# A graph attention layer on one NeuronCore: edge mask over three tables, output projection in two passes, layer norm work on three engines

## The chip, the cores and the metric

The kernel runs on one core of a Trainium2 chip. The core has a matrix engine (TensorE, in the profile PE for the matmuls and PEld for the weight loads that run beside them), a vector engine (VectorE, DVE), an activation engine (ScalarE, ACT), a general engine (GpSimd, POOL) and a queue engine (SyncE, SP) that only issues transfers. Each engine works through its own list of instructions in order; semaphores tie the lists together. Transfers are issued by SP, ACT or POOL and carried out by sixteen DMA engines.

The metric is the device time of one execution in microseconds (us). The kernel before took 323.02 us, the median of three runs of 318.78, 323.02 and 324.04 us.

## The reference, cut to what matters

```python
h = relu((x - mean(x)) / sqrt(var(x) + 1e-5))          # x: 384 tokens x 1024, float32
q, k, v = h @ wq.T + bq, h @ wk.T + bk, h @ wv.T + bv
q2, k2, v2 = q @ wiq.T + biq, k @ wik.T + bik, v @ wiv.T + biv     # 16 heads of 64
mask = full((384, 384), -inf)
mask[src, dst] = softplus(edge_type_weights)[edge_type - 1]        # 6528 edges; a later edge overwrites
mask[i, i] = w[3] where the diagonal is still -inf
attn = softmax(q2 @ k2.T / 8 + mask)                               # per head
out = x + concat_heads(attn @ v2) @ wo.T + bo
```

Seven weight matrices of 1024 x 1024 are read. A pair (source, destination) may occur several times among the edges, and the last one has to win. All is float32: each product is made of three matmuls on exact splits of both operands into a high and a low part.

## The kernel before, in words

**Tiling.** A weight matrix comes in eight chunks of 128 x 1024 (512 KB). A chunk is loaded by SP into one of three `raw` buffers (`load`, L59), its high part is made by ACT (`split_hi`, L66 to L76), its low part by DVE or POOL (`split_lo`, L78 to L81), and PE multiplies. One chunk against 384 tokens is eight times three matmuls of 128 x 384; this is called a slot. The function `slot_head` (L382) splits chunk w+2 and loads chunk w+4 while chunk w is multiplied.

**Stages, in order.** Layer norm of three token tiles with transposes (L236 to L350); projection v (slots 0 to 7), projection q (8 to 15), projection iv (16 to 23), projection k (24 to 31); then the attention stage, which has the remaining sixteen chunks (iq and ik, two for each of eight head pairs) as filler between the attention's own matmuls, followed by the output projection over the eight wo chunks.

**Layer norm.** DVE makes statistics (L244, L247), ACT and POOL subtract the mean for tiles 0 and 1 (L273, L275), DVE for tile 2 (L277), PE transposes (L285), ACT makes the high part (L291), DVE the low part (L296). DVE makes the high part of weight chunk 0 (L334), POOL its low part (L336). The factor 1/sqrt(var) is applied later, to the projections (L371), with the row made in the second slot (`ln_row`, L263).

**Mask.** Edges lie in 51 columns of 128. A key, source times 384 plus destination, is made twice: per partition (`mask_keys`) and as rows along the free axis. The rows go to memory and come back to all partitions (`key_rows`, `key_load`, L166 to L192), so that DVE can find in each column the edges that have a later twin (`mask_detect`, L206, L209). Those go to a dump cell. Each column is then written by one indirect DMA of POOL, a scatter (L221), into a table in memory of 384 x 384 cells. Scatters into one table are ordered: each waits until the one before it on the same table has landed. There are two tables, columns 0 to 25 and 26 to 50, filled at the start with the base mask and with -1 (L203, L204, issued by POOL). After the last scatter both are read back by SP (L230), and DVE overlays the second on the first (`mask_select`, L233, L234).

The order of the work is written out by hand: what stands first in the program stands first on its engine. Two of those places matter below.

```python
L489  def extra_k(m):
L492      if m == 5:
L493          mask_finish()          # SP: read both tables back, in slot 29
L676  fill(PRE)                      # three chunks of iq/ik before the attention loop
L677  mask_select()
```

**Attention loop.** One step (L679) handles one head and one tile of 128 queries: scores S (PE, L602) into one of three PSUM banks `s`; mask, scale and row maximum (DVE, L608); exponential (ACT, L612); normalisation (POOL, L620; from step 43 on DVE, L618); transpose T (PE, L625) into one of two banks `t`; the splits (ACT L634, DVE L635); and each third step the product with v (PE, L642). Step i has S(i), the mask of i-1, the transpose of i-5. Between them `fill` issues filler matmuls: 7.9 units of credit a step while iq and ik last, then 5 for the output projection, whose partial sums for five of six output tiles are collected by `fill_o` (L578) over seven chunks.

**Output.** After the loop come the last chunk for five tiles, the sixth tile in two halves over all eight chunks, the sum with x + bo (made by POOL at L719, added by DVE at L725), and the stores (L726).

Of the kernel before, what the change touches and what calls it, by code (L numbers as in the profile page):

```python
# [22 lines left out]
def gnn_kernel(ctx: ExitStack, tc: tile.TileContext, x, edges, erows, etw, wq, wk, wv, wiq, wik, wiv, wo,  # L23
               bcol, biv, bo, out):
    """h = relu(LN(x)); masked 16-head attention with doubled projections; out = x + attn @ wo.T + bo.

    float32 products run as float32r passes on exact splits a = ah + al (ah has 12 significant bits):
    a.b = ah.bh + ah.bl + al.bh, accumulated in PSUM.
    """
# [9 lines left out]
    EB = 8  # L39
    DS = 3  # L40
    WARM = (20, 0, 0, 0)

    def bank(tag):
        return psum.tile([128, 512], F32, tag=tag, name=tag, bufs={"s": 3, "a": 1}.get(tag, 2))
# [4 lines left out]
    # ------------------------------------------------------------ weights  # L49
# [9 lines left out]
    def load(w):  # L59
        if w >= NCH:  # L60
            return
        n, m = chunks[w]
        raw[w] = wpool.tile([128, D], F32, tag="raw", name="raw", bufs=3)
        nc.sync.dma_start(raw[w], W[n][m])
# [22 lines left out]
    # ------------------------------------------------------------ start: loads  # L87
# [3 lines left out]
    xn = [xall[:, (NT + t) * D:(NT + t + 1) * D] for t in range(NT)]  # L91
    for t in range(NT):
        for c in (slice(0, 512), slice(512, D)):
            nc.sync.dma_start(xt[t][:, c], x[t * 128:(t + 1) * 128, c])
    ert = work.tile([128, N], F32, tag="e", name="er", bufs=EB)
    er = ert[:EC, :256].bitcast(I32).rearrange("p (a j) -> p a j", a=2)
# [9 lines left out]
    load(2)  # L106
# [4 lines left out]
    nc.gpsimd.memset(upper, 1.0)  # L111
    nc.gpsimd.affine_select(upper, upper, pattern=[[1, 128]], compare_op=OP.is_gt, fill=0.0, base=0,
                            channel_multiplier=-1)
# [5 lines left out]
    # ------------------------------------------------------------ mask  # L119
# [7 lines left out]
    tabs = [dram.tile([CELLS + 128, 1], F32, name=f"tab{g}") for g in range(2)]  # L127
    ma = const.tile([128, NT, N], F32, name="ma")
    krow = dram.tile([EC, 128], F32, name="krow")
    mbt = {}  # L130
    SPLITC = 26

    def mask_consts():
        nc.gpsimd.iota(dump.bitcast(I32), pattern=[[0, 1]], base=CELLS, channel_multiplier=1)
        nc.gpsimd.tensor_copy(w8[:, 8:9], dump.bitcast(I32))
        nc.gpsimd.memset(ma, -3.0e38)
        for j in range(NT):
            nc.gpsimd.tensor_scalar(ma[:, j, j * 128:(j + 1) * 128], ident, 3.0e38, -3.0e38, op0=OP.mult, op1=OP.add)

    def mask_keys():  # L140
        nc.gpsimd.tensor_copy(ed.bitcast(F32), ed)
        nc.gpsimd.tensor_scalar(tmpe[:, 0, :], tmpe[:, 0, :], float(N), None, op0=OP.mult)
        nc.gpsimd.tensor_tensor(key, tmpe[:, 0, :], tmpe[:, 1, :], OP.add)

    def softplus_a():
        nc.vector.tensor_scalar(w8[:, 0:4], ew, 0.0, None, op0=OP.max)
        nc.vector.scalar_tensor_tensor(w8[:, 4:8], ew, -1.0, ew, op0=OP.mult, op1=OP.min)
        nc.scalar.activation(w8[:, 4:8], w8[:, 4:8], AF.Exp)

    def softplus_b():  # L150
        nc.scalar.activation(w8[:, 4:8], w8[:, 4:8], AF.Ln, bias=1.0)

    def softplus_c():
        nc.scalar.activation(sq, epsc, AF.Exp)
        nc.vector.tensor_tensor(w8[:, 4:8], w8[:, 4:8], w8[:, 0:4], OP.add)
        nc.vector.tensor_scalar(w8[:, 4:8], w8[:, 4:8], 8.0, None, op0=OP.mult)
# [7 lines left out]
    kf = ert[:EC, :256].rearrange("p (a j) -> p a j", a=2)  # L164

    def key_rows_a():  # L166
        nc.gpsimd.tensor_copy(kf, er)
        nc.gpsimd.tensor_scalar(kf[:, 0, :], kf[:, 0, :], float(N), None, op0=OP.mult)

    def key_rows_b():  # L170
        nc.gpsimd.tensor_tensor(krt[:EC, :128], kf[:, 0, :], kf[:, 1, :], OP.add)
        nc.gpsimd.dma_start(krow, krt[:EC, :128])

    rows = {}
    PA = 9
    sc_order = []
    for i in range(SPLITC):
        sc_order.append(i)
        if SPLITC + i < EC:
            sc_order.append(SPLITC + i)  # L180

    def parts(g):
        return [(c0 + g * PA, min(c0 + (g + 1) * PA, c1)) for c0, c1 in ((0, SPLITC), (SPLITC, EC))]

    def key_load(g):
        t = work.tile([128, 2, NT, N], F32R, tag="pt", name="rows")
        rv = t.bitcast(F32).rearrange("p a k n -> p (a k n)")
        for s, (c0, c1) in enumerate(parts(g)):
            dst = rv[:, s * PA * 128:(s * PA + c1 - c0) * 128]
            for c in range(c0, c1):  # L190
                rows[c] = rv[:, (s * PA + c - c0) * 128:(s * PA + c - c0 + 1) * 128]
            nc.gpsimd.dma_start(dst, krow[c0:c1, :].rearrange("c j -> (c j)").partition_broadcast(128))  # L192

    def mask_tables():
        neg = work.tile([128, N], F32, tag="e", name="neg", bufs=EB)
        nc.gpsimd.memset(neg, -1.0)
# [5 lines left out]
        for g, (m, col) in enumerate(((ma, ma[:, 0, 0:1]), (neg[:, None, :].to_broadcast([128, NT, N]), neg[:, 0:1]))):  # L202
            nc.gpsimd.dma_start(tabs[g][:CELLS, :].rearrange("(j p m) o -> p j (m o)", p=128, m=N), m)  # L203
            nc.gpsimd.dma_start(tabs[g][CELLS:, :], col)  # L204

    def mask_detect(c):  # L206
        """Among the 128 edges of a chunk an edge with a later twin goes to a dump cell."""
# [4 lines left out]
    def mask_index(cs):  # L212
        t0 = tmpe[:, 0, cs]
        nc.vector.tensor_scalar(t0, key[:, cs], -1.0, w8[:, 8:9], op0=OP.mult, op1=OP.add)
        nc.vector.scalar_tensor_tensor(t0, cnt[:, cs], 0.5, t0, op0=OP.is_gt, op1=OP.mult)
        nc.vector.tensor_tensor(t0, t0, key[:, cs], OP.add)
        nc.vector.tensor_copy(idx[:, cs], t0)

    def mask_scatter(i):
        c = sc_order[i]  # L220
        nc.gpsimd.indirect_dma_start(out=tabs[0 if c < SPLITC else 1],  # L221
# [3 lines left out]
    def mask_finish():  # L225
        assert nsc[0] == EC
        mbs = work.tile([128, 2, NT, N], F32R, tag="pt", name="mbs")
        mbt["m"], mbt["s"] = mbs[:, 0, :, :].bitcast(F32), mbs[:, 1, :, :].bitcast(I32)
        for g, m in enumerate((ma, mbt["m"])):
            nc.sync.dma_start(m, tabs[g][:CELLS, :].rearrange("(j p m) o -> p j (m o)", p=128, m=N))  # L230

    def mask_select():
        nc.vector.tensor_scalar(mbt["s"], mbt["m"], 0.0, None, op0=OP.is_ge)  # L233
        nc.vector.copy_predicated(ma, mbt["s"], mbt["m"])  # L234

    # ------------------------------------------------------------ layer norm, relu, transpose  # L236
# [9 lines left out]
    def ln_mean(t):  # L246
        nc.vector.bn_aggr(lnt[:, 2 * t:2 * t + 2],  # L247
                          lnt[:, 30 + 12 * t:42 + 12 * t].rearrange("p (a b) -> p a b", a=2))
        if t < 2:
            nc.vector.tensor_scalar(negm[:, t:t + 1], lnt[:, 2 * t:2 * t + 1], -1.0, None, op0=OP.mult)  # L250

    def ln_root():
        nc.scalar.activation(root, var, AF.Sqrt, bias=epsc, scale=0.25)

    def ln_rstd():
        """1/sqrt(var + eps): root = sqrt((var + eps)/4), one Heron step root + (var + eps)/4 / root, inverse"""
        nc.vector.tensor_scalar(vq, var, 0.25, EPS / 4, op0=OP.mult, op1=OP.add)
# [517 lines left out]
```

## Time and profile before

| | |
|---|---|
| runs | 318.78, 323.02, 324.04 us; median 323.02 |
| profiled execution | span 319.3 us from its first to its last instruction |
| PE busy | 295.3 us (92%) |
| PEld, DVE, ACT, POOL busy | 277.8, 197.3, 153.1, 168.7 us |
| weight matmul 128 x 384 | start to start 0.17 us in unbroken stretches |
| scatters, L221 | 51, of 1112 ns mean, between 52.4 and 153.9 us |
| DMA | 50.80 MB, mean 159 GB/s |
| granted PE clock | 0.989 mean; 0.66 between 160 and 170 us |

The page lists no further time of the profiled execution outside its span; its span lies within the range of the three runs, 3.7 us under their median. A matmul's recorded duration overlaps the next one's, so the distance from start to start is its cost. "Waits" name for each engine what ended its idle time; the "chain" follows the work that ended last back to the start.

### The profile page before, as it was taken

What the parts mean: (1) busy time and instruction counts of PE and PEld (TensorE: products, weight loads), DVE (VectorE), ACT (ScalarE), POOL (GpSimd) and SP (SyncE); (2) the same over time, 40 slices, a digit from 0 to 9 for tenths busy, and PEclk for the clock granted to TensorE, in tenths of its full rate; (3) what the DMA queues carried; (4) which work ended last, traced back from release to release, by engine and by line L of the source; (5) the groups of instructions that cost most, each with busy time, mean ns of one, the idle gap of its engine ahead of it and who ended that gap; (6) DMA issues with size and microseconds to landing.
All of it is one profiled execution on the core that took longest, in us unless ns stands there. A gap on an engine that the chain in (4) does not pass through costs nothing.

```text
span 319.3 us, 4938 instructions
## 1 busy us (share of the span) xinstructions
PE 295.3 (92%) x1655; PEld 277.8 (87%) x1655; DVE 197.3 (62%) x498; ACT 153.1 (48%) x285; POOL 168.7 (53%) x170
## 2 busy tenths in 40 slices
PE   7799999799999999999728999999999999967995
PEld 5789999689988899999728999999999998855885
DVE  3958995799633315888035457676676767896041
ACT  2846330533422224552051587777777768953100
POOL 5748941454645546557222266473747488752630
PEclk9999999999999999999968999999999999999999
DMA  7678697636553432420369776474656577432022
GB/s 215 240 224 270 197 248 224 168 129 201 191 158 124 128 124 66 132 68 0 121 249 248 189 216 171 120 190 126 180 147 192 115 231 202 164 132 66 2 101 96
DMA packets 19903, 50.80 MB, mean 159 GB/s; under 512 B 4390, under 2 KB 7642, under 8 KB 19878
## 3 DMA queue, kind: packets, MB, share of 16 engines
q1 hardware_dynamic: 17062, 45.91, 48.0%
q0 software_dynamic: 2816, 4.58, 5.4%
q8 instruction: 13, 0.21, 0.3%
q14 instruction: 12, 0.10, 0.1%
HBM read 38.23 MB, written 2.81 MB: 129 GB/s over the span
## 4 chain that ended last, share of the span: by engine, by line
PE 58%; DMA 17%; DVE 12%; POOL 5%; issue 4%; ACT 2%; SPq 1%; ACTq 0%; DVEq 0%
PE g L356 9%; PE g L358 9%; PE g L357 9%; PE s L602 5%; DMA raw<-in_wq_dram 5%; PE a L642 5%; PE t L625 4%; PE s L358 3%; PE s L357 3%; PE s L356 3%; DMA tab<-val,idx 3%; POOL tab L221 3%; DVE whl L81 3%; DVE junk L209 2%; DMA raw<-in_wik_dram 2%
## 5 line engine op out<-in xcount | busy, mean ns | idle before, releaser
L356 PE MATMUL g<-g,whl 128*128 128x384 f32 x312 | 107.8, 346 | 11.8 <-DVE nat L367 8.2
L358 PE MATMUL g<-g,whl 128*128 128x384 f32 x312 | 105.2, 337 | 0.0
L357 PE MATMUL g<-g,whl 128*128 128x384 f32 x312 | 105.0, 336 | 0.0
L221 POOL DMA_INDIRECT tab<-val,idx x51 | 56.7, 1112 | 53.2 <-DMA tab<-val,idx 28.2
L76 ACT ACTIVATE whl<-raw 128x1024 fp32r<-128x1024 f32 x50 | 52.5, 1052 | 51.6 <-PE s L358 21.1
L81 DVE TENSOR_TENSOR whl<-raw,whl 128x1024 fp32r<-128x1024 f32 x40 | 48.8, 1220 | 40.8 <-ACT whl L76 40.8
L356 PEld LDWEIGHTS g<-g,whl 128*128 128x128 f32 x312 | 59.1, 190 | 13.1 <-DVE nat L367 8.5
L357 PEld LDWEIGHTS g<-g,whl 128*128 128x128 f32 x312 | 59.3, 190 | 0.0
L358 PEld LDWEIGHTS g<-g,whl 128*128 128x128 f32 x312 | 59.1, 189 | 0.0
L620 POOL TENSOR_TENSOR e<-e,s 128x384 f32<-128x384 f32 x43 | 35.4, 829 | 38.4 <-DVE s L616 32.8
L372 ACT ACTIVATE g<-f,bc 128x384 fp32r<-128x384 f32 x24 | 14.8, 616 | 48.1 <-DVE f L371 48.1
L81 POOL TENSOR_TENSOR whl<-raw,whl 128x1024 fp32r<-128x1024 f32 x11 | 26.3, 2393 | 19.9 <-ACT whl L76 18.7
L612 ACT ACTIVATE e<-e,s 128x384 f32<-128x384 f32 x48 | 29.3, 611 | 14.4 <-DVE s L608 14.2
L635 DVE TENSOR_TENSOR pt<-t,pt 128x384 fp32r<-128x384 f32 x48 | 26.4, 552 | 8.5 <-ACT pt L634 7.7
L625 PE MATMUL t<-ident,e 128*128 128x128 f32 x144 | 23.7, 273 | 4.3 <-DVE pt L635 4.3
L634 ACT ACTIVATE pt<-t 128x384 fp32r<-128x384 f32 x48 | 23.1, 482 | 8.9 <-PE t L625 8.6
L608 DVE CUSTOM_DVE_ANT_0 e<-s,ma 128x384 f32<-128x384 f32 x48 | 26.3, 549 | 1.5 <-PE s L602 1.2
L367 DVE SCALAR_TENSOR_TENSOR nat<-g,bc,nat 128x384 fp32r<-128x384 f32 x16 | 9.9, 618 | 26.8 <-ACT nat L366 22.6
L602 PE MATMUL s<-ks,qs 128*128 128x384 f32 x96 | 25.0, 341 | 1.2 <-DMA ks<-nat 1.2
L625 PEld LDWEIGHTS t<-ident,e 128*128 128x128 f32 x144 | 18.5, 140 | 7.8 <-DVE pt L635 5.4
L642 PE MATMUL a<-pt,vhl 128*128 128x384 f32 x96 | 20.8, 351 | 0.0
L371 DVE TENSOR_TENSOR f<-g,rrow 128x384 f32<-128x384 f32 x24 | 13.2, 554 | 10.2 <-PE g L358 10.2
(152 smaller groups left out, 432.5 us busy)
## 6 DMA issues: line engine op xcount, KB each, us to landing
ks<-nat SPq DMA_DIRECT2D x32, 192.0 KB, 3.4
raw<-in_wv_dram SPq DMA_DIRECT2D x8, 512.0 KB, 5.1
raw<-in_wq_dram SPq DMA_DIRECT2D x8, 512.0 KB, 4.3
raw<-in_wiv_dram SPq DMA_DIRECT2D x8, 512.0 KB, 3.4
raw<-in_wk_dram SPq DMA_DIRECT2D x8, 512.0 KB, 3.3
raw<-in_wiq_dram SPq DMA_DIRECT2D x8, 512.0 KB, 5.3
raw<-in_wik_dram SPq DMA_DIRECT2D x8, 512.0 KB, 3.6
raw<-in_wo_dram SPq DMA_DIRECT2D x8, 512.0 KB, 4.5
```

The costliest lines, as they stand in the source:

```text
L76: nc.scalar.activation(dst[0], raw[w], AF.Copy)
L81: (eng or nc.vector).tensor_tensor(lo, raw[w], hi.bitcast(F32), OP.subtract)
L221: nc.gpsimd.indirect_dma_start(out=tabs[0 if c < SPLITC else 1], out_offset=bass.IndirectOffsetOnAxis(ap=idx[:, c:c + 1], axis=0), in_=val ...
L356: nc.tensor.matmul(ps, lhi, rhi, start=first, stop=False)
L357: nc.tensor.matmul(ps, lhi, rlo, start=False, stop=False)
L358: nc.tensor.matmul(ps, llo, rhi, start=False, stop=last)
L602: nc.tensor.matmul(ps[:, :N], qs[:, o, t * 128:(t + 1) * 128], ks[:, o, s, :], start=(s == 0), stop=(s == 1))
L612: nc.scalar.activation(es[i], es[i], AF.Exp, bias=s[:, 0:1], scale=-1.0, accum_out=s[:, 1:2])
L620: nc.gpsimd.tensor_tensor(es[i], es[i], s[:, 2:3].to_broadcast([128, N]), OP.mult)
L625: nc.tensor.transpose(ps[:, k * 128:(k + 1) * 128], es[i][:, k * 128:(k + 1) * 128], ident)
L635: nc.vector.tensor_tensor(lo, pv, hi.bitcast(F32), OP.subtract)
L642: nc.tensor.matmul(ps[:, :N], vhl[:, k, p, 2 * o:2 * o + 2, :], pts[h][:, s, k, :], start=(k == 0 and s == 0), stop=(k == 2 and s == 1))
```

## The change

Mask: three tables of 17 columns each in place of two, filled with zero by SP in slots 0 to 2; the scatters alternate over all three, two a slot, from slot 3. The base mask is made by POOL in slot 22. The keys' rows are made and read back by SP and not by POOL, and earlier. The duplicate search is spread over slots 1 to 23. The tables are read back by POOL (and not SP) in slots 29 to 31, and overlaid one each at the first three iq/ik chunks. An index needs two DVE operations and not four.

Layer norm: x in three loads and not six; the negated mean by ACT; chunk 0's high part by ACT; one of tile 2's high parts by DVE. The softplus, with its table loads, is moved ahead of the first slot. The cast of the edges (`mask_floats`) stands ahead of chunk 1's low part on POOL.

Buffers: four `raw` buffers, loads five chunks ahead; three PSUM banks `g` and two `s` (two and three before); six buffers `e` (eight before).

Attention: 84 units of filler ahead of the loop (72 before); the chunk's head (evacuation, splits, load) runs at the end of a step; the first pair's copies are half issued by ACT; all normalisation on POOL. Output projection: chunks 0 to 3 for all six tiles are summed into x + bo, which is made in slots 18 to 25 and kept in memory; chunks 4 to 7 make a second pass; 8 units of credit a step.

```diff
-    EB = 8
-    DS = 3
-    WARM = (20, 0, 0, 0)
+    EB = 6
+    NTAB, RNG = 3, EC // 3
+    JI = [0, 1, 3, 5, 8, 11, 14, RNG]
+    WARM = (20, 6, 0)
 def bank(tag):
-        ... bufs={"s": 3, "a": 1}.get(tag, 2))
+        ... bufs={"g": 3, "a": 1}.get(tag, 2))
 def load(w):
-        raw[w] = wpool.tile([128, D], F32, tag="raw", name="raw", bufs=3)
+        raw[w] = wpool.tile([128, D], F32, tag="raw", name="raw", bufs=4)
+    def table_clear(g):
+        nc.sync.dma_start(tabs[g][:CELLS, :].rearrange("(j p m) o -> p j (m o)", p=128, m=N),
+                          zero[:, None, :].to_broadcast([128, NT, N]))
+    def key_rows():
         nc.gpsimd.tensor_copy(kf, er)
+        nc.gpsimd.tensor_scalar(kf[:, :EC], kf[:, :EC], float(N), None, op0=OP.mult)
+        nc.gpsimd.tensor_tensor(krt[:, :EC], kf[:, :EC], kf[:, EC:], OP.add)
+        nc.sync.dma_start(krow.rearrange("c j -> (c j)").rearrange("(p e) -> p e", p=128), krt[:, :EC])
+    PA = 6
+    sc_order = [r * RNG + j for j in range(RNG) for r in range(NTAB)]
+    def mask_index(j0, j1):
+        k, n, i, t0 = (a.rearrange("p (r j) -> p r j", r=NTAB)[:, :, j0:j1] for a in (key, cnt, idx, tmpe[:, 0, :]))
+        nc.vector.scalar_tensor_tensor(t0, n, 2.0 * CELLS, k, op0=OP.mult, op1=OP.add)
+        nc.vector.tensor_scalar(i, t0, w8[:, 8:9], None, op0=OP.min)
-    def mask_finish():
+    def mask_load(g):
...
+        nc.gpsimd.dma_start(mbt[g], tabs[g][:CELLS, :].rearrange("(j p m) o -> p j (m o)", p=128, m=N))
-    def mask_select():
-        nc.vector.tensor_scalar(mbt["s"], mbt["m"], 0.0, None, op0=OP.is_ge)
-        nc.vector.copy_predicated(ma, mbt["s"], mbt["m"])
+    def mask_select(g):
+        nc.vector.copy_predicated(ma, mbt[g].bitcast(I32), mbt[g])
 # layer norm
-        nc.vector.tensor_copy(t0[:, 0, c], raw[0][:, c])
+        nc.scalar.activation(t0[:, 0, c], raw[0][:, c], AF.Copy)
...
-    ln_hi(2, 0, p2[0])
+    ln_hi(2, 0, p2[0], nc.vector)
...
+    softplus_a()
+    mask_floats()
     split(1, nc.gpsimd)
-    key_rows_a()
-    key_rows_b()
-    key_load(0)
+    split_hi(2)
+    softplus_b()
     mask_keys()
 def detect(s):
+        if s == 0:
+            softplus_c()
+            mask_values()
+        if s < NTAB:
+            table_clear(s)
+        if 3 <= s < 6:
+            key_load(1, s - 3)
+        if 9 <= s < 12:
+            key_load(2, s - 9)
+        detects((0, 3, 6)[s] if s < 3 else 2)
+        if s >= 3:
+            scatters(2)
 def extra_k(m):
-        if m == 5:
-            mask_finish()
+        scatters(2)
+        if m >= 5:
+            mask_load(m - 5)
+        if m < 2:
+            residual(m + 6)
+    def qk_head(w):
+        first = w - W0 < 3
+        if not first:
+            load(w + 5)
+            split_hi(w + 2)
+        if pendq:
+            pendq.pop(0)()
+        if 0 < w - W0 < NTAB:
+            mask_select(w - W0)
+        if first:
+            split_hi(w + 2)
+        split_lo(w + 2, nc.gpsimd if (w + 2) % 2 == PAR else None)
+        if first:
+            load(w + 5)
+        if w == W0:
+            mask_select(0)
-    PRE, RATE, RATE_O, RATE_E = 72, 7.9, 5, 5
+    PRE, RATE, RATE_O, RATE_E = 84, 7.9, 8, 8
-    PAR, OPOOL, ODVE, ND = 1, (2, 3, 5, 6, 7), (2, 7), 43
+    PAR, OPOOL, ODVE = 1, (2, 3, 4, 6), (2,)
+    KH = 4
 def do_norm(i):
-        if i >= ND:
-            nc.vector.tensor_scalar(es[i], es[i], s[:, 2:3], None, op0=OP.mult)
-        else:
-            nc.gpsimd.tensor_tensor(es[i], es[i], s[:, 2:3].to_broadcast([128, N]), OP.mult)
+        nc.gpsimd.tensor_tensor(es[i], es[i], s[:, 2:3].to_broadcast([128, N]), OP.mult)
 def fill_o():
+        first = [(0, 0), (0, 1), (1, 0), (1, 1), (2, 0), (2, 1)]
+        first += [(a, k) for k in (2, 3) for a in range(3)] + [(a, k) for a in range(3, 6) for k in range(KH)]
...
+            if k == KH - 1:
+                ysums.append(a)
+        todo = [(a, k) for k in range(KH, 7) for a in range(5)]
 # output, sixth tile
-        for k in range(8):
+        for k in range(KH, 8):
             omm(*OT[5], k, c)
```

## The prediction

> **What bounds the kernel now.** First the page's slices: PE is busy nearly everywhere, and its clock is full but for one place.
>
> ```profile
> PE   7799999799999999999728999999999999967995
> PEclk9999999999999999999968999999999999999999
> ```
>
> So only PE's own stops count. There are four places: the start, a dip near slice 8, a hole at slices 19 and 20 (about 157 to 166 us), a dip at slice 35 (281 to 291). The view of PE's waits gives their sizes (total, times, longest):
>
> ```profile
> PE g L356 <- DVE nat L367: 8.2, 1, 8.2
> PE t L625 <- DVE pt L635: 4.3, 3, 2.5
> PE g L356 <- DVE f L371: 3.6, 3, 2.4
> ...
> PE s L602 <- DMA ks<-nat: 1.2, 1, 1.2
> ```
>
> That is 17.3 us behind the first real matmul. DVE's L367 is only the last link of the hole; the chain, in order of time (start, length), shows its root:
>
> ```profile
> 152.90 2.13 DMA tab<-val,idx
> ...
> 155.48 0.39 SPq L230
> ...
> 157.04 6.65 DMA raw<-in_wik_dram
> ```
>
> The last scatter lands at 155.0, then SP reads the tables back, and only then does SP issue the chunk that PE needs. The view of line L230 tells how long SP's list stood (durations shortest/median/longest, first and last start):
>
> ```profile
> L230 SPq EVENT_SEMAPHORE  x2: 28/9012/17997, 137.1 to 155.9; - x2
> ```
>
> 18.0 us from 137.1, with three weight loads queued behind. PE's timeline shows a second price of the hole:
>
> ```profile
> 157.51 0.34 PE L358 MATMUL g<-g,whl 128*128 128x384 f32 x1
> 166.02 0.69 PE L356 MATMUL g<-g,whl 128*128 128x384 f32 x1 [8.18 <-DVE nat L367]
> ...
> 169.07 0.52 PE L356 MATMUL g<-g,whl 128*128 128x384 f32 x1
> 169.39 0.46 PE L357 MATMUL g<-g,whl 128*128 128x384 f32 x1
> 169.68 0.33 PE L358 MATMUL g<-g,whl 128*128 128x384 f32 x1
> ```
>
> Eleven matmuls take 3.66 us from 166.02 to 169.68; at 0.173 each they would take 1.90. The restart costs 1.76 us more, and the granted clock is 0.66 in that stretch.
>
> **Part by part.**
>
> *Mask, end.* The read-back leaves SP for POOL, whose next work is a chunk split three slots later, so no weight load stands behind it. Does the mask come in time? With two tables the 51 scatters run from 52.4 to 153.9 us, 2.0 us each; POOL's own part is 0.96 + 0.30. With three tables an equal pace is the upper bound, 1.3 the lower. The fill of table 0 is in SP's slot 0, so the first scatter can go at about 30 us; the last nine need slot 23's indices, at about 114 us. By the slow pace the last lands at 30 + 51 x 2.0 = 132, or 114 + 18 = 132; a read-back takes 3.9 (the row of ma<-tab), so about 137. DVE asks for the first at the head of slot 32, at 22.7 + 30 x 4.15 = 147 us. Ten us of cover. The three overlays cost DVE 1.54 each (L234) instead of 0.76 + 1.54: with a low part of 1.22 and an evacuation of 0.62 that is 3.4 of a slot's 4.15. Gone are 8.2 + 1.76. The ks wait of 1.2 goes as well: 84 - 72 = 12 units put four more triples, 2.1 us, ahead of the first S.
>
> That pair's copies are half issued by ACT. [...] I count 0: the extra filler already covers it, and ACT's four issues, some 2 us, stand in a stage where ACT is half idle.
>
> *Mask, early.* DVE's duplicate search goes from five columns a slot (0.275 us each, DVE over 9.7 of 10 us between 30 and 50) to two: 2.7 us of a slot. The two later waits on L371 (2.9 us together) came with a wq chunk that was 15.5 us on its way between the table fills and the key rows. After, fills and rows are in SP's own list. From 12 us, ahead of chunk 8 come seven chunks (3.67 MB), rows (1.18) and three fills (1.77), 6.6 MB: at 212 GB/s, the rate in the saturated stretch from 40 to 50 us, 31 us, so 43; chunk 8 is due at 22.7 + 6 x 4.15 = 47.6 less 2.4 for its split. Covered by 2 us; at 190 GB/s it is 1 to 3 us late. I take 0, and 3 for the range. The later SP steps (six loads and stores of x + bo, about one of each a slot) put a store's wait of some 2.3 us before one load a slot, with four buffers ahead: 0.
>
> *Layer norm and start.* Before, slot 2 starts at 21.54. The second half of x tile 1 lands at 7.36; now both statistics (0.69 each) follow it, one more than before, so ACT's high parts come 0.6 later, at 11.8. ACT then casts half of chunk 0 (half of 1.05), so POOL's low part starts at 12.3 and takes 2 x 1.30; then comes the cast of the edges, which POOL did later:
>
> ```profile
> 13.87 2.40 POOL L81 TENSOR_TENSOR whl<-raw,whl 128x1024 fp32r<-128x1024 f32 x1
> 15.01 1.28 DVE L257 TENSOR_SCALAR lnt<-lnt 128x3 f32<-128x3 f32 x1
> 24.96 1.07 POOL L141 CAST ed<-ed 128x153 f32<-128x153 int32 x1
> ```
>
> The low part of chunk 1, 16.27 at its end before, is then done at 12.3 + 2.6 + 1.07 + 2.40 = 18.4 (before, POOL reached it at 13.87). Slot 1's third matmul needs it: 18.4 + 22 x 0.173 + 0.5 for the row = 22.7, against 21.54: +1.2. This contains the first L371 wait (0.7), which the third g bank takes away. Lower bound: no wait at all, 20.8 (-0.7). [...] DVE's subtraction of tile 2 (0.44 a half) now stands beside POOL's key rows (0.35 + 0.55 + 0.30). [...] Since slot 1 waits for POOL and not for DVE, I take +1.2 and set 2.4 as the upper end. Softplus ahead of slot 1 puts three table loads (1.28 each) before ACT's row and first evacuation: some 23.5 us; slot 3 needs that bank at 27. No cost.
>
> *Attention.* Until 281 us PE never stops, so nothing is to be had there; the chunk heads at the step's end change the order only. The 4.3 us at 281 to 291 come from DVE:
>
> ```profile
> 280.71 2.35 POOL L81 TENSOR_TENSOR g<-raw,g 128x1024 fp32r<-128x1024 f32 x1 [0.81 <-ACT g L76]
> 280.73 2.54 DVE L618 TENSOR_SCALAR e<-e,s 128x384 f32<-128x384 f32 x1
> ```
>
> L618 takes 0.42 alone and 2.5 beside a POOL split; five take 7.2 us. On POOL five normalisations are 5 x 0.83 = 4.1 us, one split less gives back 2.4: POOL has room (4.7 of 10 us there). DVE loses 7.2 and gains six sums of 0.69 and one low part of 1.22. Eight credits give two triples of 0.68 us a step, so a step grows by about 0.5 us and the chains have more cover: in the built order eleven triples lie between the last S and the last T, and six (4.1 us) between the last product with v and chunk 7, which waits for 0.49 + 0.55 + 0.52 + 1.01 = 2.6. I take 3.8 of the 4.3. In all the passes hold the same matmuls; only the sixth tile's half chunks move (24 x 0.120 for 12 x 0.227): 0.
>
> **Sum**, from the span: 319.3 - 8.2 - 1.76 - 1.2 - 2.9 - 3.8 + 1.2 = 302.6. The profile has no time outside its span, which is at the low end of the runs and 3.7 under their median. What part of that offset stays is not known: 0 gives 302.6, all of it 306.3. As the hole that could vary is gone, I take 1.4: **304.0 us**.
>
> **Rivals.**
> 1. *The start and the feed are late* (0.14): slot 2 at 2.4 instead of 1.2, a chunk or two late by 3 each, clock loss with it: 304 + 1.2 + 3 to 7 = 308 to 312. For it: the first 50 us move nearly all fills, rows and chunks through one list. Against it: up to 254 GB/s in an unsaturated stretch (20 to 30 us).
> 2. *The mask is still late* (0.09): one wait takes the other's place, DVE's overlay, with PE's evacuations queued behind. It needs a pace above (147 - 4 - 30)/51 = 2.2 us, against 2.0. At 2.4 it lands 9 us late and the clock price returns: 304 + 11 = 315. This is also "the change doesn't do what it says".
> 3. *Slower: two s banks* (0.06). S(i) must wait for DVE's L608 of i-2. In steps of 2.3 us that is 4.6 us; from S to the end of L608 it is mostly 1.2 to 3.6 us, but up to 4.95 (S at 246.9, L608 to 251.87), where DVE had an evacuation and a split in between. If the lag passes two steps in every step, 48 steps lose one L608 of 0.55 each: +26, 330 us. It decides from a lag of two steps on; against it, the heads now stand behind L608.
>
> My forecast has 0.71. "Faster" holds the forecast, rival 1 and half of rival 2; 2% of 323.02 (316.6 and 329.5), about what a measurement of this kernel can tell from no change, are the bounds. Range: 299 (no start cost, no offset, all of 4.3) to 312.
>
> **What would show it.** PE's waits without nat L367; SP without a long L230; clock 1.00 from 150 to 175; the last scatter by 135; slot 2 near 22.7; no stop over 1 us from 281 on. Wrong if PE waits for L713's s bank, if DVE stands at the overlay, or if `raw` loads land over 10 us after issue in the first 60 us.

## The result, and the profile after

The changed kernel takes 300.53 us (median of four runs, 300.45 to 302.02), the kernel before 322.59 (318.78 to 324.04; a fourth run of 322.16 has joined the three named at the top): a ratio of 0.936, 95% interval 0.930 to 0.942. Now and then a run of one kernel comes out slower, at a lower granted clock; the ratios here leave such runs out, so they need not equal the quotient of the medians. The forecast was 304.0 with a range of 299 to 312. The profiled execution took 300.52 us, with a span of 298.8; so 1.7 us lie outside the span.

The slices of the page of the kernel after, in 40 parts:

```profile
PE   6999999999999999999999999999999999999995
PEclk9999999999999999999999999999999999999999
```

The 7, 2 and 8 at slices 19 to 21 (counted from 0) are gone, the 6 and 7 near the end too, and so is the dip in the clock. The view of what PE waited for (in total, times, longest), whole:

```profile
PE g L311 <- POOL ident masks.py:199: 1.4, 1, 1.4
PE s L291 <- ACT g L279: 1.1, 1, 1.1
PE g L291 <- DVE g L283: 0.5, 1, 0.5
```

All three lie ahead of the first product, in the layer norm. Of the 17.3 us of waits behind it the view lists none any more. The windows of the after profile over the stretch of the hole and of the tail (us, busy time of each engine, clock, DMA share, GB/s):

```profile
150.00:160.00 10.00, 10.00 (x59) 10.00 (x58) 6.21 (x6) 5.00 (x6) 3.67 (x2) 1.00 0.79 197
160.00:170.00 10.00, 10.00 (x60) 9.97 (x60) 5.79 (x19) 5.39 (x14) 5.41 (x5) 1.00 1.01 264
...
280.00:290.00 10.00, 10.00 (x49) 8.36 (x48) 1.93 (x4) 1.50 (x3) 1.02 (x1) 1.00 0.00 0
```

PE is busy for 10.00 of every 10.00 us at clock 1.00; the kernel before had 7.84 and 3.98 in the first two of these windows, and 0.66 as its clock in the second. And the mask, by the lines of the scatters and of the read-backs (durations shortest/median/longest, first and last start):

```profile
L227 POOL DMA_INDIRECT tab<-val,idx x51: 953/959/1900, 26.7 to 124.6; - x51
...
L236 POOL DMA_DIRECT2D mbs<-tab x3: 746/780/842, 125.6 to 128.2; - x3
```

The last scatter starts at 124.6, before at 152.9. DVE's overlays come at 148.12 and stand for nothing:

```profile
148.12 1.54 DVE L240 COPY_PREDICATED ma<-mbs 128x1152 f32<-128x1152 int32 x1
149.61 0.62 DVE L381 SCALAR_TENSOR_TENSOR nat<-g,bc,nat 128x384 fp32r<-128x384 f32 x1
150.14 1.54 DVE L240 COPY_PREDICATED ma<-mbs 128x1152 f32<-128x1152 int32 x1
```

Where the 20.5 us of span went: slot 2 starts at 20.36 instead of 21.54 (1.2); from slot 2 to the last matmul's start it is 274.65 us instead of 294.19 (19.5); behind that 3.8 instead of 3.6.

### The profile page after: what moved, and what is told of

Same layout as the page of the kernel before. It is cut to its first block, busy times and chain, and to the rows that moved or that the text cites. A ratio compares the mean times of both kernels' runs of the same rounds, so it can differ in the third digit from the quotient of the medians.

```text
span 298.8 us, 4985 instructions
## 1 busy us (share of the span) xinstructions
PE 292.2 (98%) x1657; PEld 276.6 (93%) x1657; DVE 198.8 (67%) x492; ACT 155.3 (52%) x290; POOL 156.3 (52%) x163
## 4 chain that ended last, share of the span: by engine, by line
PE 95%; DMA 2%; DVE 1%; SPq 0%; issue 0%
PE g L372 22%; PE g L370 22%; PE g L371 21%; PE s L707 6%; PE a L744 6%; PE t L727 5%; DMA g<-in_x_dram 2%; PE s L371 2%; PE s L372 2%; PE s L370 2%; PE g L419 2%; PE t L372 2%; PE t L371 2%; PE t L370 2%; PE a L372 1%; PE a L371 1%
## 5 line engine op out<-in xcount | busy, mean ns | idle before, releaser
L371 PE MATMUL g<-g,whl 128*128 128x384 f32 x312 | 104.2, 334 | 0.0
L77 ACT ACTIVATE whl<-raw 128x1024 fp32r<-128x1024 f32 x51 | 53.5, 1051 | 29.9 <-PE g L372 21.1
L722 POOL TENSOR_TENSOR e<-e,s 128x384 f32<-128x384 f32 x48 | 39.2, 828 | 38.1 <-DVE s L721 29.7
L371 PEld LDWEIGHTS g<-g,whl 128*128 128x128 f32 x312 | 58.7, 188 | 0.0
L82 DVE TENSOR_TENSOR whl<-raw,whl 128x1024 fp32r<-128x1024 f32 x41 | 50.3, 1227 | 11.9 <-ACT whl L77 10.2
L381 DVE SCALAR_TENSOR_TENSOR nat<-g,bc,nat 128x384 fp32r<-128x384 f32 x16 | 9.9, 618 | 15.1 <-ACT nat L380 13.1
```

The lines of the kernel that those rows point to most:

```text
L77: nc.scalar.activation(dst[0], raw[w], AF.Copy)
L82: (eng or nc.vector).tensor_tensor(lo, raw[w], hi.bitcast(F32), OP.subtract)
L371: nc.tensor.matmul(ps, lhi, rlo, start=False, stop=False)
L722: nc.gpsimd.tensor_tensor(es[i], es[i], s[:, 2:3].to_broadcast([128, N]), OP.mult)
```

## Experiments: what removed the hole

The prediction gave the hole to SP's list: SP stood 18 us at the read-back with three weight loads behind it. Three things in the change bear on it: the read-back leaves SP, the scatters start at 27 instead of 52 us, and they go to three tables. In all that follows the edit is to the kernel named, the rest is as it stands. Ratios are to the kernel before on the chip of the run, where its medians were 318.4, 320.7 and 318.3 us. The kernel after was not run again on these three chips. Versions in whose profile PE has no wait behind the first product took 300.4 on the first, 300.6 and 301.5 on the second and 300.6 on the third, so a difference to the kernel after's 300.53 holds across chips to about 1 us.

**The read-back moved alone, in the kernel before.**

```diff
-            nc.sync.dma_start(m, tabs[g][:CELLS, :]...
+            nc.gpsimd.dma_start(m, tabs[g][:CELLS, :]...
```

> The kernel before, with one line changed: the two tables are read back by POOL and not by SP. Theory (the hole at 157 us is SP's list standing behind the read-back): the last scatter still lands near 155 us and the mask near 160, but the three weight loads behind it go out near 137; the 8.2 us wait and the slow clock behind it (1.8) go, 312 to 313 us against 322.6. Rival (the scatters have to end earlier, so three tables are needed): DVE stands at the overlay from 157 until the mask is there, PE stops at the attention's first steps, and less than 3 us are won.

Measured: 316.13 us against 318.36, ratio 0.997 (0.991 to 1.003): no difference that counts. PE's waits in this version:

```profile
PE s L602 <- DMA ks<-nat: 6.0, 1, 6.0
PE t L625 <- DVE pt L635: 4.4, 3, 2.6
```

The wait on nat L367 is gone, as expected, and the weight loads go out in time. But a stop of 6.0 us has come in its place, on the copies of the first q2/k2 pair. It is no shorter than the hole is in some executions: in the version with only the normalisation moved (`b_norm_pool`, further down), whose mask is untouched, the wait on nat L367 was 5.5 us. Its timeline (start, length, engine and line, with the idle time before in brackets) shows what they run into:

```profile
154.23 0.80 POOL L230 DMA_DIRECT2D ma<-tab  x1 [1.68 <-DMA tab<-val,idx]
...
155.02 0.81 POOL L230 DMA_DIRECT2D mbs<-tab  x1
...
156.67 2.91 SPq L521 DMA_DIRECT2D ks<-nat  x4
...
164.30 0.76 DVE L233 TENSOR_SCALAR mbs<-mbs 128x1152 int32<-128x1152 f32 x1 [4.95 <-DMA mbs<-tab]
...
166.48 0.98 PE L602 MATMUL s<-ks,qs 128*128 128x384 f32 x2 [5.97 <-DMA ks<-nat]
...
167.26 0.52 PE L356 MATMUL g<-g,whl 128*128 128x384 f32 x1
167.58 0.52 PE L357 MATMUL g<-g,whl 128*128 128x384 f32 x1
```

Both read-backs go out at 154 to 156, right ahead of the copies; those need until 166.4, and the mask is late for DVE as well. Behind the stop the matmuls come 0.32 us apart instead of 0.17: the second price is paid again. So SP's list gave the hole its form in the kernel before, and was not its root.

**The opposite: the read-back given back to SP, in the kernel after.**

```diff
-        nc.gpsimd.dma_start(mbt[g], tabs[g][:CELLS, :]...
+        nc.sync.dma_start(mbt[g], tabs[g][:CELLS, :]...
```

> The kernel after, with its three tables read back by SP. Theory: either of the two edits is enough; the scatters end at 126 us, SP reaches the read-backs at about 131 and does not stand, so the time stays at 300.5 with no wait on PE over 0.5 us. Rival (taking the read-back off SP is what counts): SP stands again and PE has a hole of several us, 305 us or more.

Measured: 300.42 us (300.10 to 301.99), ratio 0.948 (0.940 to 0.957). No stop of PE at the mask. With the scatters over at about 126 SP has nothing to stand for at its read-backs (134.0 to 142.3). Taking the read-back off SP is neither enough (316.1) nor needed (300.4).

**Scatters put later in the program.**

```diff
-        if s >= 3:
+        if s >= 8:
             scatters(2)
...
-        scatters(2)
-        if m >= 5:
-            mask_load(m - 5)
+        scatters(3 if m >= 5 else 2)
+        if m == 7:
+            for g in range(NTAB):
+                mask_load(g)
```

> The changed kernel with its scatters begun five slots later (slot 8 instead of 3, still two a slot), so that the last is issued in slot 31 at about 142 to 147 us instead of 124.6; the three read-backs stay on POOL, at the end of slot 31. What is computed stays the same. Theory A (what removed the hole is that the scatters end early): the read-backs go out at 147 to 150, land at 154 to 160, fall onto the copies of the first q2/k2 pair, and DVE, which asks for the overlay at 148, stands 5 to 9 us; three g banks and the triples ahead cover some of it. PE stops 3 to 8 us in the stretch from 150 to 170: 303.5 to 311 us. Theory B, the prediction's (the hole was SP's list, with the weight loads queued behind the read-back): the list is free, DVE stands but PE has filler and banks enough: within 1.5 us of the changed kernel, 300 to 302.

> The same late scatters (slot 8 to 31), and the three read-backs issued by SP as before. What is computed stays the same. Theory A: SP stands until the last scatter has landed, about 148, with the loads of slots 32 on behind it, but four raw buffers are ahead; 1 to 4 us more than the late scatters with POOL's read-back: 305 to 314 us. Theory B: the hole of before returns in full, 8 us and the 1.8 us of half clock: 309 to 312 us, while the version with POOL's read-back stays at 300 to 302. The pair of runs gives the price of SP's list by itself.

Measured: 301.45 us (300.35 to 302.33) with POOL's read-back, 300.63 (300.19 to 302.60) with SP's. Both numbers would speak for theory B, but the profile takes that away: the edit didn't make the scatters late. Their line in the first of the two:

```profile
L227 POOL DMA_INDIRECT tab<-val,idx x51: 952/959/2009, 27.2 to 126.4; - x51
```

27.2 to 126.4, as in the kernel after. POOL has hardly other work in slots 3 to 8, and its list isn't tied to PE's slots: it takes the next scatter as soon as its indices are there and its table's last scatter has landed (of its waits at this line 14.2 us are for landings, 8.1 and 3.9 for DVE's search and indices). The two runs say nothing on a late mask. They show that the place of a step in the program was not what set its time here, and serve as further runs of the kernel after on another chip.

**Two tables instead of three.**

```diff
-        nc.gpsimd.indirect_dma_start(out=tabs[c // RNG],
+        nc.gpsimd.indirect_dma_start(out=tabs[i % 2],
```

> The changed kernel with the scatters alternating over two tables; the third stays at zero and is still read back and merged, so the order of overwriting between edges is not kept, all else is. Theory A (the early end comes from the early start and from two scatters a slot, not from the third table): two tables run at 2.0 us a scatter by before's profile, a slot of 4.15 us holds two of them, so the last lands at 126 to 134 us and the time stays within 1 us of the changed kernel, 300 to 301.5. Rival (the third table is needed): POOL, which stands in order at each scatter, delays its splits of the odd chunks, PE waits for low parts, 302 to 306; or the mask ends past 150 and DVE stands at the overlay, 305 or more.

Measured: 306.36 us (303.05 to 308.61), ratio 0.957 (0.945 to 0.969). Theory A fell, by a step of mine that came from the profile of before: I took its pace of 2.0 us a scatter along. The scatters' line and POOL's wait for them (in total, times, longest):

```profile
L227 POOL DMA_INDIRECT tab<-val,idx x51: 952/960/1995, 27.0 to 149.8; - x51
```

```profile
POOL tab L227 <- DMA tab<-val,idx: 49.0, 28, 3.8
```

That is (149.8 - 27.0)/50 = 2.46 us a scatter; 49 us in which POOL waits for a landing, against 11.0 with three tables. The median time from issue to landing was 2.6 us in the kernel before; here it is 3.8. So with two tables the early start alone does not bring an early end. The profiled execution is the slowest of the four, so its stops are read for what they are, not for their size; DVE, ACT and PE in the timeline:

```profile
156.68 1.55 DVE L240 COPY_PREDICATED ma<-mbs 128x1152 f32<-128x1152 int32 x1 [6.73 <-DMA mbs<-tab]
...
158.13 0.60 DVE L381 SCALAR_TENSOR_TENSOR nat<-g,bc,nat 128x384 fp32r<-128x384 f32 x1
...
158.76 0.51 ACTq L563 DMA_DIRECT2D qs<-nat  x1
159.31 0.83 ACTq L565 DMA_DIRECT2D qs<-nat  x1
...
160.18 1.06 ACT L77 ACTIVATE whl<-raw 128x1024 fp32r<-128x1024 f32 x1 [9.15 <-issue]
...
161.29 0.44 PE L370 MATMUL g<-g,whl 128*128 128x384 f32 x1 [2.60 <-ACT whl L77]
...
163.72 0.59 PE L372 MATMUL g<-g,whl 128*128 128x384 f32 x1 [1.82 <-POOL whl L82]
```

This is the chain of rival 2, with a link that I had not seen: DVE stands 6.73 us at the overlay, the low part of the first pair's q stands behind it (L381), ACT's two copies wait for that, and ACT's next high part (L77) stands 9.15 us behind its own copies. PE's stop carries the name of ACT, which only passes the wait on. The prediction counted ACT's issues at nothing; that holds only while the mask is in time. One of the four runs took 303.05 us, so the price differs from run to run.

**Two tables, and the read-back on SP.** Both edits above together.

> The version whose scatters alternate over two tables (last scatter at 149.8 us, read-backs behind it, 306.4 us in its runs), with the read-backs issued by SP as before. The order of overwriting between edges is not kept, all else is. Theory A2 (with a late mask SP's list is a price of its own): SP stands at the read-back from about 141 to 152, chunks 35 and 36 are issued behind it and PE's hole of before returns: 2 to 6 us over the version with POOL's read-back, 308 to 312 us, with a long wait on a chunk's load in the trace. Rival (once the mask is late, the overlay on DVE is the price, whoever issues the read-back; the five chunks loaded ahead cover SP's stand): 305 to 307.5 us.

Measured: 305.97 us (302.72 to 306.72), ratio 0.959 (0.951 to 0.967), as with POOL's read-back within the spread of the runs. What SP, DVE and PE waited for, and the first pair's copies:

```profile
SPq L236 <- DMA tab<-val,idx: 12.9, 1, 12.9
```

```profile
DVE ma L240 <- DMA mbs<-tab: 2.2, 2, 1.3
```

```profile
PE s L707 <- issue: 4.4, 1, 4.4
```

```profile
155.72 2.02 ACTq L572 DMA_DIRECT2D ks<-nat  x2
155.78 2.80 SPq L572 DMA_DIRECT2D ks<-nat  x2
```

SP stands 12.9 us before its read-backs (145.7 to 147.7), and the loads behind them come late. PE's list ends at 160.14 and starts again with the first S at 164.87, 4.73 us, with the DMA engines full between (shares 1.06 and 1.01 in the two windows of ten us from 150 on). In the kernel after the same copies are issued from 154.4 on, all four by 156.6, and S starts at 160.18 without a stop; here it starts 9.1 us after the first of them. The view of PE's waits names no releaser for the stop; the view of the tile `ks` has the weight load of S waiting 4.7 us for the copies.

So the rival had the right number by another mechanism: DVE stood only 2.2 us for the overlays here, and what PE missed were the copies. SP's stand is real, as theory A2 had it, but it did not make the kernel slower than POOL's read-back does. The pair doesn't hold all else equal, since the last scatter was issued at 143.6 us here and at 149.8 there. What it shows is that with a late mask PE stops with either issuer, at another link of the chain.

What follows from the six: **the end of the scatters decides.** With the last scatter issued at about 125 us the read-back can be on either engine (300.5 and 300.4); with the last at 143.6 to 152.9 there is a hole with either (306.0 and 306.4 in the kernel after, 318.4 and 316.1 in the kernel before). And the early end needs the third table besides the early start. That the early start is needed too is argued only: taking it back alone was tried and did not come off, as told above. At the pace of three tables, (124.6 - 26.7)/50 = 1.96 us, a first scatter at 52.4 us would put the last at about 150 (an estimate), where the other versions have their hole.

## Experiments: the start, the s bank, the tail and the feed

**x in six half loads again, in the kernel after.**

```diff
-        nc.sync.dma_start(xt[t], x[t * 128:(t + 1) * 128, :])
+        for c in (slice(0, 512), slice(512, D)):
+            nc.sync.dma_start(xt[t][:, c], x[t * 128:(t + 1) * 128, c])
```

> The kernel after, with x loaded in six halves as before. The start came 2.3 us earlier than predicted (slot 2 at 20.4 and not 22.7). Theory A (three whole loads land earlier than six halves): x tile 1 lands near 7.4 again and slot 2 starts at 21.5 to 22.5, 1 to 2 us slower. Theory B (the rest of the new start order does it): slot 2 stays within 0.4 us of 20.4.

Measured: 301.93 us (300.59 to 302.27), ratio 0.953 (0.943 to 0.962). The statistics of x tile 1 in this version, and after them in the kernel after (timeline of DVE):

```profile
7.91 0.69 DVE L251 BATCH_NORM_STATS2 lnt<-g 128x6 f32<-128x512 f32 x1 [1.76 <-DMA g<-in_x_dram]
```

```profile
5.70 1.23 DVE L250 BATCH_NORM_STATS2 lnt<-g 128x6 f32<-128x512 f32 x2
```

With whole loads the tile is there by 5.70, and DVE doesn't wait for it. With halves its second one comes at 7.91, and the first product starts at 12.36 instead of 10.85. The profile shows the mechanism; the medians lie 1.4 apart, but the runs of both kernels fall into the same two groups, near 300.5 and near 302 (last section), so the size rests on one profile of each: spans of 300.1 and 298.8 us.

**The chunk heads run where the filler meets them, not at the step's end.**

```diff
                 tasks.append(lambda w=w: qk_head(w))
-                if now[0] < 0:
-                    run_tasks()
+                run_tasks()
```

> The changed kernel with the heads of the q2/k2 chunks run where the filler comes to them, not gathered at the step's end; two s banks as in the changed kernel. Theory A (the slack behind the s bank was only 0.06 us at its smallest, so the deferral is what makes two banks do): DVE's evacuation and low part (some 1.8 us) fall ahead of L713 in up to 16 steps, S of two steps later waits for it by 0.5 to 1.5 us in about half of them: PE waits for s of 4 to 12 us in total, 304 to 312 us. Rival (the third g bank and the filler between give the slack, the order doesn't matter): no wait over 1 us, 300 to 301.5 us.

Measured: 310.40 us (309.43 to 311.48), ratio 0.974 (0.964 to 0.984): 9.9 us over the kernel after. PE's waits, then one of the places in the timeline:

```profile
PE s L706 <- DVE s L712: 6.8, 7, 1.6
```

```profile
222.49 0.62 DVE L381 SCALAR_TENSOR_TENSOR nat<-g,bc,nat 128x384 fp32r<-128x384 f32 x1 [3.32 <-ACT nat L380]
...
223.03 1.22 DVE L82 TENSOR_TENSOR whl<-raw,whl 128x1024 fp32r<-128x1024 f32 x1
...
224.16 0.55 DVE L712 CUSTOM_DVE_ANT_0 e<-s,ma 128x384 f32<-128x384 f32 x1
...
224.77 0.61 PE L706 MATMUL s<-ks,qs 128*128 128x384 f32 x2 [1.22 <-DVE s L712]
```

An evacuation and a low part, 1.84 us, stand ahead of the line that frees the s bank, and S waits for it. From that line's end (224.71) to S (224.77) it is 0.06 us. In the kernel after three of the 48 S start at that distance too (at 191.3, 206.1 and 263.5 us), so there the two banks have no slack left; PE's stops at them are 0.12 to 0.15 us, too short for the view. Theory A held: with two s banks the deferral of the heads is worth about ten us, of which the view of waits places 6.8.

**The last normalisations on the other engine**, once in each kernel. Before, with `ND` from 43 to 99 (all on POOL):

> The kernel before, with the last five normalisations on POOL too. Theory (DVE stands beside POOL's splits): PE's 4.3 us of waits for pt fall to under 1.5, about 3 us faster. Rival (PE runs out of filler there, whoever normalises): the waits stay at 3 us or more, no change.

Measured: 316.09 us, ratio 0.997 (0.992 to 1.002). In the trace the tail's waits of 4.3 us became `PE t L625 <- POOL e L620: 1.9, 1, 1.9`; 2.4 us were won, less than the runs can tell. After, from step 43 on back on DVE:

```diff
-        nc.gpsimd.tensor_tensor(es[i], es[i], s[:, 2:3].to_broadcast([128, N]), OP.mult)
+        if i >= 43:
+            nc.vector.tensor_scalar(es[i], es[i], s[:, 2:3], None, op0=OP.mult)
+        else:
+            nc.gpsimd.tensor_tensor(es[i], es[i], s[:, 2:3].to_broadcast([128, N]), OP.mult)
```

> The changed kernel with the last normalisations (from step 43 on) on DVE again, as before. Theory (DVE's tensor_scalar stands beside a POOL split for its whole length, about 2.5 us instead of 0.42, and T waits for it; the same taken from the kernel before won 2.4 us in the trace): 1 to 3 us slower, 301.5 to 303.5, with waits for pt of 1 to 3 us behind 280 us. Rival (eight credits a step and the second pass give so much cover that DVE's place no longer matters): 300 to 301.2, no wait over 0.6 us.

Measured: 300.64 us (300.48 to 302.13), ratio 0.947 (0.942 to 0.953): no loss, the theory fell. The line of these five on DVE, and what POOL had beside them:

```profile
L723 DVE TENSOR_SCALAR e<-e,s x5: 420/422/709, 268.2 to 276.3; 128x384 f32<-128x384 f32 x5
```

```profile
270.37 2.43 POOL L82 TENSOR_TENSOR g<-raw,g 128x1024 fp32r<-128x1024 f32 x1 [3.11 <-ACT g L77]
```

They take 0.42 to 0.71 us; the longest of the kernel before took 2.57. Only one split is left on POOL in that stretch, and only the normalisation at 272.35 (0.68) meets its end; the one of 0.71, at 276.34, stands beside a sum of POOL. By these rows the long normalisations beside a split were gone, with the splits in their new places.

**Five credits a step for the tail instead of eight.**

```diff
-    PRE, RATE, RATE_O, RATE_E = 84, 7.9, 8, 8
+    PRE, RATE, RATE_O, RATE_E = 84, 7.9, 5, 5
```

> The changed kernel with five credits a step for the output projection and the tail instead of eight, as before. Theory (the chains of the last steps need the triples between them): steps are 0.5 us shorter, S to T waits 0.3 to 1 us in several steps behind 250 us, the triples left over stand at the end: 301.5 to 304 us. Rival (with the normalisation on POOL the chain is short enough by itself): 300 to 301.2 us.

Measured: 308.02 us (307.59 to 309.33), ratio 0.970 (0.964 to 0.976): 7.5 us, twice the top of what I expected. PE's waits of this version:

```profile
PE a L744 <- DVE aof L755: 2.7, 1, 2.7
...
PE t L727 <- DVE pt L737: 1.1, 4, 0.4
...
PE a L744 <- DVE pt L737: 0.6, 1, 0.6
```

PE stands in four steps between 264 and 274, then 2.75 and 0.55 us on the last chain; behind that the matmuls come at about half rate:

```profile
283.79 0.63 PE L372 MATMUL g<-whl,g 128*128 128x512 f32 x1
284.21 0.63 PE L370 MATMUL g<-whl,g 128*128 128x512 f32 x1
...
286.51 0.39 PE L370 MATMUL g<-g,g 128*128 128x512 f32 x1
286.74 0.40 PE L371 MATMUL g<-g,g 128*128 128x512 f32 x1
```

0.43 from start to start until 285.9, 0.23 from 286.3 on; the granted clock is 0.83 from 280 to 290. The triples that would have covered the stops stand at the end. So the tail is held by the credits, that is by the filler between the chains, not by the engine of the normalisation.

**Three raw buffers instead of four** (`bufs=4` to `bufs=3`).

> The changed kernel with three raw buffers instead of four, all else as it is, so that SP stands at a chunk's load until the split three chunks earlier has ended. Theory (the prediction's step: the feed is covered, the fourth buffer is only reserve): 300 to 301.5 us. Rival (the early feed is covered by the fourth buffer alone): loads of slots 5 to 12 come late behind fills and key rows, PE stops 1 to 5 us there, 302 to 306 us.

Measured: 303.12 us (302.28 to 305.93), ratio 0.956 (0.949 to 0.963), 2.6 us slower in the medians (1.8 in the profiled execution, the fastest of the four), but not where the rival looked for it. Until 110 us PE is as full as in the kernel after, and slot 2 starts no later. The two stops are at 119.3 (0.65 us) and at 160.7 (1.0, the first S waiting for its copies). SP stands at the loads (in total, times, longest):

```profile
SPq L65 <- DVE whl L82: 102.9, 32, 4.3
SPq L65 <- POOL whl L82: 32.9, 10, 4.4
```

With 42 such waits, 135.8 us in all (in the kernel after the first line has 68.6 in 22), whatever is behind a load in SP's list slips, the first pair's copies among it. The fourth buffer is no help in the first 50 us and pays at the start of attention.

None of these versions beats the kernel after by more than its own spread.

## Why the prediction was right, and where it was wrong

The time came out 3.5 us below the forecast. In terms of the sum (span 302.6 forecast, 298.8 measured):

- **Start, +1.2: wrong, it was -1.2.** This is the largest error, 2.4 us. I let x tile 1 arrive at 7.36 as before; with whole loads it is there by 5.70, which I had not counted although the diff shows it. The run with half loads has it at 7.91 and the first product 1.5 us later. The second part was the cast of the edges, put down at 1.07 by its row of before; in the new place it took 0.32. The low part of chunk 1 ended at 15.97 instead of the 18.4 worked out, so slot 1 never waited for it: slot 1 starts 0.35 us earlier than before, and the wait at the head of slot 2, 0.85 us from start to start, is gone. The upper end of 2.4, which rival 1 takes up, was the author's estimate: up to 1.2 us more for DVE's subtraction of tile 2 beside POOL's key rows. No run shows that term: both of DVE's halves (L283) took 0.88 us together, from 9.40 on, and POOL's key rows had ended at 9.38.
- **Hole, -8.2 and -1.76: right in size, wrong in its root.** The stop is gone whole, and no half-rate stretch is left. But the step "no weight load stands behind it" isn't what did it. The read-back alone on POOL left a hole of 6.0 us and the half rate; the prediction's own check "does the mask come in time?" was the real argument, and its times (last scatter by 132, mask at 137, DVE at 147) came out as 128 at the latest, when the third read-back is issued, some 130 to 137 for the mask (an estimate: issued from 125.6 to 128.2, with the 4.4 to 8.7 us from issue to landing of the version with late scatters and POOL's read-back), and 148. Luck had a part in it. The pace of 2.0 us a scatter was called an upper bound from the kernel before, where a scatter landed after 2.6 us in the median; in the changed kernel it lands later (3.7 to 4.2 in nine of its versions, last section), and two tables then need 2.34 to 2.46 us a scatter. Three tables came out at 1.96, at the bound and not well below it.
- **ks wait, -1.2, and L371's waits, -2.9: right.** Start to start they were 1.4 and 3.3. The cover of chunk 8 held, and even three raw buffers cost nothing there. Which part of the change removed L371's waits is not shown: no run took back the third `g` bank or the new places of the fills and key rows. They also differ from one execution of the kernel before to the next, 3.6 us in its profile and 1.2 in that with the read-back on POOL. That ACT's share of the first pair's copies saves nothing was not tested either; its four issues, put at some 2 us (an estimate from SP's rows of before, 0.46 to 0.60 us an issue), took 3.3 together in the kernel after.
- **Tail, -3.8 of 4.3: gone whole, for one reason of the two.** Measured from start to start it was 4.8, 1.0 more than counted. The credits carry it (7.5 us when taken back). The normalisation on POOL, from which I counted 7.2 us off DVE, is worth nothing in the kernel after that the runs can tell: with the splits where they now are, DVE's five take 0.42 to 0.71 us. In the kernel before it won 2.4 us in the trace. One cure was enough.
- **Offset, 1.4 of 3.7: about right.** In every run whose time and span are both listed, 1.7 us lie outside the span. If that held for the profiled execution of the kernel before too, 1.7 of the 3.7 was that, and the rest its spread.

Of the rivals, the late start and feed did not come: slot 2 was early, and PE waited for no chunk. The late mask is real with two tables. Its price was oversized: 11 us forecast for 9 us of lateness, 5.3 in the median of the runs without the slowest, since PE had work on hand: in the profiled execution DVE stood 7.7 us for the overlays, PE 4.4 by its waits, and the half rate behind it took 1.7 more. The point from which it decides (2.2 us a scatter) fits: at 1.96 it did not come, at 2.34 and 2.46 it did. The rival with two s banks is real too, at its place and by its mechanism; but only steps near a chunk's head pay, 9.9 us and not 26, so it would not have made the kernel slower than before.

## What to carry to other kernels

When a hole has several links (a late landing, a list that stands, an engine that waits), moving one link can move only the name of the wait; look for what all of them wait for, and ask when that ends. Two cures of one wait don't add: count the cover once, then see what is left for the other. And before a step is moved in the program, see what its engine's list waits for: where it waits for data and not for its turn, the move changes nothing.

## What the runs showed of the hardware

- **The start has two forms, some 1.6 us apart.** The runs of one kernel fall near 300.5 or near 302.0. In the shorter form the first transposes of the layer norm come 0.11 us apart, in the longer one 0.21, with the first product at 10.85 and 12.54 us. PE's timeline of the kernel after:

```profile
6.83 0.66 PE L291 MATMUL s<-ident,g 128*128 128x128 f32 x4 [1.12 <-ACT g L279]
```

  and in the version with late scatters and POOL's read-back, where they come at the same time and take nearly twice as long:

```profile
6.85 1.11 PE L291 MATMUL s<-ident,g 128*128 128x128 f32 x4 [0.89 <-ACT g L279]
```

  By the single starts the rate doubles at 5.1 us in the first (0.21 apart up to there, 0.11 behind it) and at about 10.5 us in the second. Of the eleven profiled executions of the changed kernel and its versions, eight have the short form and three the long one, with the change at about 10.5 and 10.7 us in two of these. The granted clock is given as 1.00 in both forms, and both run the same instructions up to there. What sets the time of the change no run shows.
- **A stop of PE costs more than its length only at times.** After stops of 8.2 (before), 6.0 (read-back on POOL), 2.60 + 1.82 (two tables), 4.7 (two tables, read-back on SP) and 2.75 + 0.55 us (five credits) matmuls ran at about half rate, for some 3.5 us in four of the five and 5.0 with the read-back on POOL. The half rate does not always start with the restart: with five credits the five matmuls of the product with v behind the second stop took 1.04 us from start to start (six take 1.13 in the steps before), and only then did the weight matmuls come 0.43 us apart. The kernel before had a wait of 2.5 us in its tail without it. In the versions with two tables and with five credits it followed two shorter stops close behind one another, with one or two matmuls between. What length of stop brings it was not shown. In the version with two tables three of four runs have a clock of 0.989 to 0.994 and take 305.8 us and more, the fourth has 1.00 and takes 303.05.
- **A scatter's landing is not a constant.** From issue to landing the median was 2.6 us in the kernel before and 3.7 to 4.2 in nine versions of the changed kernel, with two tables and with three alike; in the one with two tables it was as long from 52 to 100 us (4.1) as in the early slots (4.0). The DMA engines were busier: a share of 0.43 from 50 to 150 us in the kernel before, 0.63 from 27 to 127 in the kernel after. No run isolates that as the cause. A pace read from one kernel isn't that of another.
